# Last pair of a conditioned block: one block product is made last, in PSUM banks of its own, and added to the tokens in two gated parts

## The chip, the cores and the metric

The kernel runs on one core of one Trainium2 chip. The metric is the device time of one execution in microseconds (us). The profile is one execution of its own, and its rows count from the start of its span.

## What is computed

The reference takes 32 batches of 128 tokens with 512 features, a conditioning vector for each batch and a mask. The first half (normalise, modulate, two small networks, gated sum) changes the few masked tokens alone. The second half is for all tokens, and the change lies in it:

```
shift_mlp, scale_mlp, gate_mlp = jnp.split(silu(t) @ ffada_w + ffada_b, 3, axis=1)
ff_norm = _layernorm(x) * (1.0 + scale_mlp[:, None]) + shift_mlp[:, None]
h = gelu(ff_norm @ ff_w1 + ff_b1, approximate=True)      # 512 -> 1024
return x + gate_mlp[:, None] * (h @ ff_w2 + ff_b2)       # 1024 -> 512
```

All of it is float32.

## The kernel before

The tokens are taken in four pairs of groups. A pair p has two sides of four batches: side 0 and side 1. Both matrix products of a pair are done with seven block products instead of eight (Strassen's method in Winograd's form): P1 to P7, with sums and differences of blocks before and after. The first product (512 to 1024) is itself cut into seven such streams, 1, 2, 5, 6, 3, 7, 4, so that a step is named by stream and product: `7P5`. Its results, behind GELU, lie in `ha` (side 0) and `hb` (side 1); each has two halves of the inner dimension.

The second product (`SecondProduct`) has for each column block c (0 or 1, written U and V in the names of steps; 256 token columns, two tiles i of 128 each) two PSUM banks: e (`banks[c][0]`, P5, P2 and P3) and a (`banks[c][1]`, P1, P6, P7 and P4). A step such as `P2V1` is `multiply("P2", 1, 1)`: four matmuls of 128x256 into half a bank. The first half of the output columns of side 0 is bias + P1 + P2, the others are sums of more products:

- `sa`, `se` seed the banks a and e with the bias or its difference; `P1` goes into a, `P5` into e.
- `k5` copies e (P5) out on ScalarE; `ke` copies a (bias + P1) into e; `P2` is added there; e is then the first half of side 0.
- `K00c` copies e to SBUF on ScalarE, `G00c` multiplies it by the gate and `R00c` adds it to the tokens, both on GpSimd (POOL).
- `F`, `B`, `T`, `U` are the operand sums on VectorE. `B` makes the operand of P6. `U` (`fourth_block`) makes the operand of P3, and it overwrites the operand of P2, so that it stands behind P2.
- P3, P7 and P4 are cut a second time into seven inner products, p1 to p7, of 128 columns. Step `5i3` is inner product p5 of P3. `S1` to `S4` are operand sums on POOL, `C` copies on ScalarE, `V` and `J` sums on VectorE. The direct ones (2, 3, 4) go straight into the banks.
- `E0`, `E1`, `E20`, `E21` (`third`) set e to a + P5. Results for side 1 and for the other halves follow: `G11c`, `R11c`, `G10c`, `R10c` on VectorE for side 1, `K01c`, `G01c`, `R01c` on ScalarE and POOL for side 0. In these names the digits are side, half of the columns, c.
- `o00`, `o10` (c, side) store both halves of side 0 from SyncE; `o01`, `o1R`, `o1L` store side 1.

At the very end of the last pair, `4i40` and `4i41` (`last_quarter`) make the last 128 columns for one tile each, in a bank of their own, with a gate, an addition and a store of 64 KB each.

What runs first is an order written out by hand, one for each pair (`ORDER`): the names of the steps in the order in which they are issued. Each engine takes its own instructions in that order and waits by semaphores only where data, a bank or a buffer demands it. Weights for the first product and gates are loaded by SyncE (`W3`, `W4`, `lg0`, `lg1`), in that order too. Behind the last step every engine reads the number of masked tokens left over (`values_load`) and branches past a loop that isn't taken here. `SyncE` then waits for the stores.

Of the kernel before, what the change touches and what calls it, by code (L numbers as in the profile page):

```python
# [9 lines left out]
F32 = mybir.dt.float32  # L10
# [4 lines left out]
ALU = mybir.AluOpType  # L15
# [7 lines left out]
def kernel(  # L23
# [81 lines left out]
    early = ExitStack()  # L105
# [364 lines left out]
    for j, op in enumerate((ALU.is_gt, ALU.is_ge)):  # L470
        nc.gpsimd.affine_select(
            out=upper[:, j],
# [11 lines left out]
        out=lower,  # L484
# [56 lines left out]
    for j in range(2):  # L541
# [4 lines left out]
            start=True,  # L546
            stop=True,
# [34 lines left out]
    for key, vec in (("ssm1", ssm_b1), ("bwd1", bwd_b1), ("ff1", ff_b1)):  # L582
        n = vec.shape[0] // P
# [80 lines left out]
    part = KC // 2  # L664
# [233 lines left out]
    fw2_of = Weights(fw2, HC // 2, D // 2, t_2)  # L898
# [22 lines left out]
    INNER = ("P3", "P7", "P4")  # L921
# [135 lines left out]
    class FirstProduct:  # L1057
# [207 lines left out]
    class SecondProduct:  # L1265
# [55 lines left out]

        def fourth_block(self, c):
            tok, part = self.cols[c], self.ha[:, HC // 2 :]
            nc.vector.tensor_tensor(part[:, :, tok], part[:, :, tok], self.s1[c], ALU.subtract)

        def gated(self, c, side, h, result=None):

# [94 lines left out]
        def last_quarter(self, i):  # L1422

            c = 1
            part = ps_t.tile([P, 512], F32, tag="tr", name=f"last_{i}")[:, :P]
            self.inner[INNER[-1]].multiply("p4", part.unsqueeze(1), True, (i,))
            gate = self.gate[1][:, 2 * c + i, :P]
            nc.vector.tensor_tensor(part, part, gate, ALU.mult)
            xt = self.xs[1][c][:, i, :P]
            nc.vector.tensor_tensor(xt, part, xt, ALU.add)  # L1430
            nc.sync.dma_start(out[(2 * self.p + 1) * G + 2 * c + i, :, :P], xt)

        def store_part(self, lo, hi):
            c = 1
            b = (2 * self.p + 1) * G + 2 * c
            nc.sync.dma_start(
                out[b : b + 2, :, lo:hi].rearrange("b s d -> s b d"), self.xs[1][c][:, :, lo:hi]
            )

    class Inner:  # L1440
# [183 lines left out]
    class Steps:  # L1624
# [14 lines left out]
    def windows(put, q, f, first, last):  # L1639
# [50 lines left out]
        for w in range(first, last):  # L1690
# [70 lines left out]
            ng1121  # L1761
        """,
        3: """
            6P5 5P3 5P7 6P1 5j22 6c5 3P5 6w12 3c5 3P1 6w22 5P4 6s 6P2 5k12 5k21 6k11 6P6 W3 7P5 7P1
            7c5 6e 3w22 6a11 3s 6P7 6P3 6k12 7s 3P2 3P6 3w12 6a12 7P6 7P2 3k11 6j22 7w12 3e 6P4 3P7
            7k11 6a22 7e W4 6j21 4P5 3P3 7P7 7P3 4c5 3k12 F00 6a21 3j22 7w22 4P1 se1 7k12 L11 7j22
            g1222 4s 3P4 7P4 4P2 3j21 L22 se0 4P6 L12 lg0 4w12 7j21 g1221 sa1 F02 4k11 P5U0 g2211 4e
            P5U1 4P7 P1V1 4w22 k50 4j22 L21 sa0 P1U0 g2122 4P4 g2222 4j21 B0 P1U1 g22L 4P3 F12 P1V0
            g2121 ke0 F10 P5V1 4k12 P5V0 B1 T1 k51 P2U0 P2U1 T0 ke1 g2212 P2V0 K000 P2V1 G000 K001
            U0 P6V0 P6U0 R000 lg1 U1 S1i3 5i3 G001 S2i3 1i3 C1i3 S1i7 C5i3 P6V1 6i3 5i7 V6i3 P6U1  # L1770
            C5i7 1i7 C1i7 S3i3 7i3 E0 J30 S2i7 C7i3 R001 S4i3 6i7 2i3 3i3 K010 V7i3 V6i7 S3i7 S1i4
            J70 7i7 S4i7 V7i7 G010 C7i7 5i4 3i7 2i7 E1 J31 1i4 S3i4 S2i4 C1i4 J71 4i3 E20 C5i4 R010
            6i4 K011 S4i4 o00 4i7 G110 R110 V6i4 J40 7i4 E21 V7i4 G111 G011 3i4 C7i4 R011 2i4 J41
            R111 G100 R100 o10 o1R o01 G101 R101 o1L 4i40 4i41
        """,
    }
    seconds, stats = {}, {}
# [1 line left out]
    for p in range(NP):  # L1779
        more_pairs = p + 1 < NP  # L1780
        steps = Steps()
        put = steps.put
# [110 lines left out]
        put("ke0", second.seed_e, 0)  # L1893
        put("B0", second.second_block, 0)
        put_moves(0)
        if p == 0:
# [2 lines left out]
        put_blocks(1)  # L1899
        multiply("P5", 1)  # L1900
        put("k51", second.keep_five, 1)
        put("ke1", second.seed_e, 1)
        put("B1", second.second_block, 1)
        put_moves(1)
        put("T0", second.third_block, 0)
# [36 lines left out]
        join("P7", 0)  # L1942
        direct("P3", "p3")
        second.finish(put, 0, 0, 1, 0)
        put("o00", second.store, 0, 0)
# [5 lines left out]
        put("o10", second.store, 1, 0)  # L1951
        if more_pairs:
            for j in range(1, 5):
                put(f"A{j}", begin, j)
# [10 lines left out]
        put("E21", second.third, 1)  # L1965
        second.finish(put, 1, 1, 1, 0)
        if not more_pairs:
            put("o1R", second.store_part, D // 2, D)
        join("P4", 1)
        next_phases("P5", "P1")  # L1970
        if p + 2 < NP:
# [2 lines left out]
        second.finish(put, 0, 1, 0, 1)  # L1974
        put("o01", second.store, 0, 1)
        next_phases("P2", "P6")
        if more_pairs:
            for n in range(4):
                put(f"nt1{n}", nxt.token_sums, 1, n)
            direct("P4", "p4")  # L1980
            second.finish(put, 1, 1, 0, 1)
            put("o11", second.store, 1, 1)
        else:
            second.finish(put, 1, 1, 0, 1)
            put("o1L", second.store_part, P, D // 2)
            for i in range(2):
                put(f"4i4{i}", second.last_quarter, i)
        if more_pairs:
            put("nW2", nxt.load_weights, 2)
            if p + 2 < NP:  # L1990
# [16 lines left out]
    with tc.If(more > 0):  # L2007
# [11 lines left out]
        with tc.For_i(0, more, 1):  # L2019
# [12 lines left out]
            for half_no, (mod, was, wbs, bias, bcol, func) in enumerate(  # L2032
# [28 lines left out]
                out=out_rows,  # L2061
# [56 lines left out]
```

## Time and profile before

| | us |
|---|---|
| median of 3 runs | 449.38 (448.76 to 450.94) |
| the profiled execution, its own time | 448.01 |
| its span, first to last instruction | 446.3 |
| TensorE busy in the span | 435.6 |
| VectorE, ScalarE, GpSimd busy | 328.0, 205.5, 260.5 |

A row of a timeline or of a chain has the start and the duration in us, the engine (PE is TensorE, PEld its weight loads, DVE VectorE, ACT ScalarE, SP SyncE; a q behind it is that engine's queue), the line of the kernel, and what is written from what. `x8` are eight records; a float32 matmul leaves two. A row of a group has the count, the busy time, the mean ns of one, and the idle time ahead of it with what ended it. A row of a windows table has the length of the stretch, the busy time of PE, PEld, DVE, ACT and POOL, the granted clock of TensorE, and the share and GB/s of the DMA engines.

### The profile page before, as it was taken

What the parts mean: (1) busy time and instruction counts of PE and PEld (TensorE: products, weight loads), DVE (VectorE), ACT (ScalarE), POOL (GpSimd) and SP (SyncE); (2) the same over time, 40 slices, a digit from 0 to 9 for tenths busy, and PEclk for the clock granted to TensorE, in tenths of its full rate; (3) what the DMA queues carried; (4) which work ended last, traced back from release to release, by engine and by line L of the source; (5) the groups of instructions that cost most, each with busy time, mean ns of one, the idle gap of its engine ahead of it and who ended that gap; (6) DMA issues with size and microseconds to landing.
All of it is one profiled execution on the core that took longest, in us unless ns stands there. A gap on an engine that the chain in (4) does not pass through costs nothing.

```text
span 446.3 us, 7040 instructions
## 1 busy us (share of the span) xinstructions
PE 435.6 (98%) x2435; PEld 372.8 (84%) x2435; DVE 328.0 (73%) x592; ACT 205.5 (46%) x453; POOL 260.5 (58%) x226
## 2 busy tenths in 40 slices
PE   8999999999999999999999999999999999999992
PEld 4884684688888999888889998888899988888991
DVE  5788898879998589969762699697627993535174
ACT  3133116353585662536636835356477254652120
POOL 4211470089932895898528927985286618912991
PEclk9999999999999999999999999999999999999997
DMA  7999449895185307741574087416550553311014
GB/s 251 374 395 409 173 88 315 299 359 143 35 182 86 111 1 273 279 141 42 142 166 72 1 296 255 140 41 151 92 135 1 189 189 106 123 29 76 0 49 145
DMA packets 57045, 70.90 MB, mean 159 GB/s; under 512 B 34741, under 2 KB 36109, under 8 KB 55983
## 3 DMA queue, kind: packets, MB, share of 16 engines
q1 hardware_dynamic: 51742, 67.72, 48.1%
q0 software_dynamic: 3008, 2.15, 1.8%
q10 hardware_dynamic: 2256, 0.54, 0.7%
q8 instruction: 21, 0.34, 0.3%
q14 instruction: 18, 0.14, 0.1%
HBM read 56.71 MB, written 13.70 MB: 158 GB/s over the span
## 4 chain that ended last, share of the span: by engine, by line
PE 95%; DVE 2%; POOL 1%; issue 0%; ACT 0%; DVEq 0%
PE a_m L1155 20%; PE e_m L1155 16%; PE a_o L1387 12%; PE e_o L1387 12%; PE one_P L1473 7%; PE po_s L222 6%; PE ph_s L205 5%; PE a_o L1473 4%; PE e_o L1473 2%; PE five_P L1473 2%; PE ph_s L681 2%; PE a_m_alone L1155 1%; PE pm_ss L308 1%; PE pm_f L308 1%; PE part_s L342 0%; PE pl_s L255 0%
## 5 line engine op out<-in xcount | busy, mean ns | idle before, releaser
L1349 POOL TENSOR_TENSOR t<-t,gate 128x512 f32<-128x512 f32 x16 | 23.1, 1444 | 61.4 <-ACT t L1343 57.3
L1182 POOL TENSOR_TENSOR ha<-p_m,ha 128x512 f32<-128x512 f32 x20 | 25.9, 1295 | 48.7 <-DMA tw<-t_rows 23.0
L968 ACT ACTIVATE xT<-xT,modT 128x128 f32<-128x128 f32 x112 | 46.4, 487 | 8.1 <-DMA xT<-xn 8.1
L1207 DVE TENSOR_TENSOR hb<-a_m,hb 128x512 f32<-128x512 f32 x40 | 27.4, 686 | 15.7 <-PE a_m L1155 12.1
L1125 ACT ACTIVATE hb<-hb,biasT 128x256 f32<-128x256 f32 x64 | 28.3, 499 | 15.0 <-DVE hb L1207 14.7
L904 POOL DMA_INDIRECT x<-x_rows,slot_i x24 | 29.3, 1219 | 7.4 <-issue 5.7
L1197 ACT COPY ha<-e_m 128x512 f32<-128x512 f32 x32 | 18.5, 586 | 31.9 <-PE e_m L1155 31.2
L1387 PE MATMUL a_o<-t,s 128*128 128x256 f32 x128 | 29.6, 380 | 0.0
L1387 PE MATMUL a_o<-fw,ha 128*128 128x256 f32 x128 | 29.6, 379 | 0.0
L1387 PE MATMUL e_o<-fw,s 128*128 128x256 f32 x128 | 29.1, 379 | 0.0
L222 PE MATMUL po_s<-w,h_s 128*128 128x512 f32 x64 | 28.4, 594 | 0.0
L1387 PE MATMUL e_o<-fw,ha 128*128 128x256 f32 x128 | 28.3, 379 | 0.0
L1169 ACT COPY p_m<-e_m 128x512 f32<-128x512 f32 x27 | 15.7, 582 | 26.7 <-PE e_m L1155 26.6
L1387 PEld LDWEIGHTS e_o<-fw,ha 128*128 128x128 f32 x128 | 24.4, 190 | 3.3
L1387 PEld LDWEIGHTS e_o<-fw,s 128*128 128x128 f32 x128 | 24.3, 190 | 3.3
L1387 PEld LDWEIGHTS a_o<-fw,ha 128*128 128x128 f32 x128 | 24.4, 190 | 3.3
L1182 POOL TENSOR_TENSOR hb<-p_m,hb 128x512 f32<-128x512 f32 x20 | 26.2, 1313 | 1.5 <-DVE hb L1207 1.2
L1387 PEld LDWEIGHTS a_o<-t,s 128*128 128x128 f32 x128 | 23.7, 191 | 2.9
L1125 ACT ACTIVATE ha<-e_m,biasT 128x256 f32<-128x256 f32 x48 | 20.0, 469 | 12.6 <-PE e_m L1155 12.0
L1398 DVE TENSOR_TENSOR e_o<-a_o,p_o 128x512 f32<-128x512 f32 x16 | 11.0, 695 | 20.1 <-PE a_o L1387 19.0
L1155 PE MATMUL a_m<-xT,tw 128*128 128x256 f32 x96 | 24.6, 379 | 0.0
L1188 DVE TENSOR_TENSOR e_m<-a_m,ha 128x512 f32<-128x512 f32 x20 | 13.9, 696 | 14.5 <-PE a_m L1155 5.1
(275 smaller groups left out, 1151.3 us busy)
## 6 DMA issues: line engine op xcount, KB each, us to landing
x<-in_x_dram SPq DMA_DIRECT2D x16, 512.0 KB, 6.4
tw<-t_rows SPq DMA_DIRECT2D x16, 512.0 KB, 3.6
gate<-gate_rows SPq DMA_DIRECT2D x8, 1024.0 KB
out_dram<-x SPq DMA_DIRECT2D x15, 512.0 KB, 4.4
xT<-xn SPq DMA_DIRECT2D x104, 64.0 KB, 2.1
tw<-t_rows SPq DMA_DIRECT2D x16, 384.0 KB
ada_f<-in_L_cond_ffada_w_dram SPq DMA_DIRECT2D x4, 768.0 KB, 14.7
ada_a<-in_L_cond_ada_w_dram SPq DMA_DIRECT2D x4, 512.0 KB, 3.7
```

The lines of the kernel that those rows point to most:

```text
L205: nc.tensor.matmul(ph[:, :n], w[:, k, ts(f, P)], xT[:, k, :], start=(k == 0), stop=(k == KC - 1))
L222: nc.tensor.matmul(po, h[f][:, ts(i, P)], w[:, f, :], start=(f == 0 and seeded is None), stop=(f == HC - 1), skip_group_check=seeded is no ...
L904: nc.gpsimd.indirect_dma_start(out=xs[i // G][i % G // 2][:, i % 2], out_offset=None, in_=x1_rows, in_offset=bass.IndirectOffsetOnAxis(ap= ...
L968: nc.scalar.activation(out, src, AF.Identity, bias=shift, scale=scale)
L1125: nc.scalar.activation(dst[:, n], src[:, n], AF.Gelu_apprx_tanh, bias=biasT[:, f : f + 1])
L1155: nc.tensor.matmul(bank[:, ts(n, QT)].rearrange("p (i b c) -> p i b c", i=2, c=R), self.w_block(j, product)[:, ts(n, P)], self.x_block(j, ...
L1182: nc.gpsimd.tensor_tensor(self.place(RESULT[j], c), self.p5[j], other, ALU.add)
L1197: nc.scalar.copy(self.place(RESULT[j], c), src)
L1207: nc.vector.tensor_tensor(dst, a, other, ALU.add)
L1349: nc.gpsimd.tensor_tensor(view, view, self.gate[side][:, 2 * c : 2 * c + 2, part], ALU.mult)
L1387: nc.tensor.matmul(bank[:, ts(i, D // 2)], src[:, k, ts(i, P)], w[:, k, :], start=False, stop=True, skip_group_check=True,)
L1473: nc.tensor.matmul(out[:, i % out.shape[1]], src[:, k, ts(i, P)], w[:, k, :], start=(start and (i == 0 or out.shape[1] == 1) and k == 0), ...
```

## The change

It concerns the last pair alone (`NP - 1`); the other pairs issue what they did.

- P2 isn't added to e any more. `ke0` and `ke1` go. In their place `K000` and `K001` copy bias + P1 out of bank a, and `G00c`, `R00c` gate it and add it to the tokens.
- `fourth_block` writes the operand of P3 over that of P1, so that the operand of P2 stays.
- P2 goes into banks of its own (`late`): `P2U0` and `P2U1` into one, `P2V0` and `P2V1` into one each. `H` multiplies by the gate and `M` adds to the tokens, on VectorE: `H00`, `M00` for both tiles of c = 0; `H10`, `M10`, `H11`, `M11` for one tile of c = 1 each.
- The first half of side 0 has stores of its own: `q00` (256 KB) and `q10` (128 KB) from SyncE, `q11` (128 KB) from ScalarE's queue. `o00` and `o10` store the second half, 256 KB each.
- `last_quarter` goes; its product is the direct step `4i4`, and `o1L` stores the whole half.
- The order of the last pair is a new one from its first step on.

```diff
         def fourth_block(self, c):
             tok, part = self.cols[c], self.ha[:, HC // 2 :]
-            nc.vector.tensor_tensor(part[:, :, tok], part[:, :, tok], self.s1[c], ALU.subtract)
+            nc.vector.tensor_tensor(
+                self.operand("P3")[:, :, tok], part[:, :, tok], self.s1[c], ALU.subtract
+            )
...
-                "P1": self.ha[:, :hh], "P2": self.ha[:, hh:], "P3": self.ha[:, hh:],
+                "P1": self.ha[:, :hh], "P2": self.ha[:, hh:],
+                "P3": self.ha[:, :hh] if self.p == NP - 1 else self.ha[:, hh:],
...
+        def late(self, c, i):
+            if c == 0 or i:
+                pool, tag = ((ps_h, "h"), (ps_t, "tr"))[c]
+            else:
+                pool, tag = ps_o, "o"
+            if i == 0 or c:
+                self.own["late", c, i] = pool.tile([P, 512], F32, tag=tag, name=f"late_{c}_{i}")
...
+            for k in range(HC // 2):
+                nc.tensor.matmul(
+                    bank,
+                    src[:, k, ts(i, P)],
+                    w[:, k, :],
...
+        def late_gated(self, c, i):
+            view, gate, _ = self.late_parts(c, i)
+            nc.vector.tensor_tensor(view, view, gate, ALU.mult)
+        def late_added(self, c, i):
+            view, _, xt = self.late_parts(c, i)
+            nc.vector.tensor_tensor(xt, view, xt, ALU.add)
+        def finish_late(self, put, c, i, queue):
+            put(f"H{c}{i}", self.late_gated, c, i)
+            put(f"M{c}{i}", self.late_added, c, i)
+            put(f"q{c}{i}", self.store_part, c, 0, 0, D // 2, (0, 1) if c == 0 else (i,), queue)
...
+        def early(c):
+            if more_pairs:
+                put(f"ke{c}", second.seed_e, c)
+            else:
+                second.finish(put, c, 0, 0, 1)
...
         3: """
...
+            6P5 5P7 6c5 5P3 5j22 3P5 5k12 6w12 6P1 6s 3P1 5P4 6P2 3c5 5k21 6P6 W3 6w22 7P1 6k11 6e
...
+            g2222 P1U1 4e P1U0 se1 4P7 P1V1 P1V0 g22L K000 4j22 4P4 F02 4j21 se0 K001 4P3 P5U1 F12
+            g2122 G000 R000 g2121 P5U0 k50 F10 4k12 P5V0 T0 P5V1 T1 B0 B1 g2212 P6U1 U1 U0 S1i3 P2U0
+            P2U1 5i3 C5i3 S2i3 1i3 C1i3 S1i7 P6V0 5i7 G001 C5i7 lg1 H00 S3i7 R001 6i3 1i7 S2i7 k51
+            P6U0 V6i3 E0 C1i7 P6V1 J30 E1 S3i3 6i7 7i3 S4i3 S4i7 3i3 C7i3 2i3 V6i7 V7i3 J31 7i7 M00
+            V7i7 q00 K010 C7i7 J70 S1i4 4i3 S2i4 5i4 1i4 C1i4 J71 4i7 6i4 K011 E21 C5i4 3i7 G111 2i7
+            V6i4 S3i4 7i4 G011 P2V1 R111 E20 J40 V7i4 G010 C7i4 G110 S4i4 2i4 3i4 R011 J41 o1R 4i4
+            H11 P2V0 R010 o00 R110 M11 G100 R100 G101 o10 q11 R101 H10 M10 o01 o1L q10
```

More of the change, by code (lines that the diff above doesn't have):

```diff
@@ L1420, in join @@
             nc.vector.tensor_tensor(bank, bank, self.inner[product].d[:, c], ALU.add)
[L1422 to L1437, printed above, removed]
+        def late(self, c, i):
[5 more added lines that the diff above has]
+                self.own["late", c, i] = pool.tile([P, 512], F32, tag=tag, name=f"late_{c}_{i}")
+            at = i if c == 0 else 0
+            bank = self.own["late", c, 0 if c == 0 else i][:, ts(at, D // 2)]
+            w = fw2_of.of["P2"]
+            src = self.operand("P2")[:, :, self.cols[c]]
+            for k in range(HC // 2):
[3 more added lines that the diff above has]
+                    w[:, k, :],
+                    start=(k == 0 and at == 0),
+                    stop=True,
+                    skip_group_check=True,
+                )
@@ new lines, in late_parts @@
+        def late_parts(self, c, i):
+            tiles = slice(2 * c, 2 * c + 2) if c == 0 else slice(2 * c + i, 2 * c + i + 1)
+            view = self.own["late", c, i][:, : (tiles.stop - tiles.start) * D // 2]
+            here = slice(tiles.start - 2 * c, tiles.stop - 2 * c)
+            return (
+                view.rearrange("p (i d) -> p i d", d=D // 2),
+                self.gate[0][:, tiles, : D // 2],
+                self.xs[0][c][:, here, : D // 2],
+            )
+        def late_gated(self, c, i):
+            view, gate, _ = self.late_parts(c, i)
+            nc.vector.tensor_tensor(view, view, gate, ALU.mult)
@@ new lines, in late_added, with store_part @@
+        def late_added(self, c, i):
[5 more added lines that the diff above has]
+            put(f"q{c}{i}", self.store_part, c, 0, 0, D // 2, (0, 1) if c == 0 else (i,), queue)
+        def store_part(self, c, side, lo, hi, tiles=(0, 1), queue=nc.sync):
+            b, n = (2 * self.p + side) * G + 2 * c + tiles[0], len(tiles)
+            queue.dma_start(
+                out[b : b + n, :, lo:hi].rearrange("b s d -> s b d"),
+                self.xs[side][c][:, tiles[0] : tiles[0] + n, lo:hi],
@@ L1763 @@
         3: """
[L1764 to L1774, printed above, removed]
+            6P5 5P7 6c5 5P3 5j22 3P5 5k12 6w12 6P1 6s 3P1 5P4 6P2 3c5 5k21 6P6 W3 6w22 7P1 6k11 6e
+            7P5 6P3 6a11 3s 6P7 7c5 3w22 7s 3P2 3w12 7P6 6k12 6j22 6P4 W4 7P2 6a12 3k11 3P6 7k11
+            6j21 6a22 4P5 7w12 7w22 4P1 7e 7P7 3e 7j22 3P7 3j22 7P3 L11 L22 7P4 6a21 lg0 3P3 7k12
+            4c5 L12 4s 7j21 3P4 F00 4w12 L21 3j21 4w22 sa0 4P2 3k12 4k11 sa1 g1222 g2211 4P6 g1221
+            g2222 P1U1 4e P1U0 se1 4P7 P1V1 P1V0 g22L K000 4j22 4P4 F02 4j21 se0 K001 4P3 P5U1 F12
[5 more added lines that the diff above has]
+            H11 P2V0 R010 o00 R110 M11 G100 R100 G101 o10 q11 R101 H10 M10 o01 o1L q10
         """,
@@ L1878, in next_phases, with store_first_side @@
                     nxt.phase(lambda name, *args: put("n" + name, *args), 1, product)
+        def early(c):
[3 more added lines that the diff above has]
+                second.finish(put, c, 0, 0, 1)
+        def store_first_side(c):
+            if more_pairs:
+                put(f"o{c}0", second.store, c, 0)
+            else:
+                put(f"o{c}0", second.store_part, c, 0, D // 2, D)
         put("lg0", second.load_gate, 0)
@@ L1892 @@
         put("k50", second.keep_five, 0)
-        put("ke0", second.seed_e, 0)
+        early(0)
         put("B0", second.second_block, 0)
@@ L1901 @@
         put("k51", second.keep_five, 1)
-        put("ke1", second.seed_e, 1)
+        early(1)
         put("B1", second.second_block, 1)
@@ L1944 @@
         second.finish(put, 0, 0, 1, 0)
-        put("o00", second.store, 0, 0)
+        store_first_side(0)
         apart("P7", "p7")
@@ L1950 @@
         second.finish(put, 1, 0, 1, 0)
-        put("o10", second.store, 1, 0)
+        store_first_side(1)
         if more_pairs:
@@ L1967 @@
         if not more_pairs:
-            put("o1R", second.store_part, D // 2, D)
+            put("o1R", second.store_part, 1, 1, D // 2, D)
         join("P4", 1)
@@ L1976 @@
         next_phases("P2", "P6")
+        direct("P4", "p4")
+        second.finish(put, 1, 1, 0, 1)
         if more_pairs:
@@ L1979 @@
                 put(f"nt1{n}", nxt.token_sums, 1, n)
-            direct("P4", "p4")
-            second.finish(put, 1, 1, 0, 1)
             put("o11", second.store, 1, 1)
         else:
[L1984 to L1987, printed above, removed]
+            put("o1L", second.store_part, 1, 1, 0, D // 2)
+            for c, i, queue in ((0, 0, nc.sync), (1, 0, nc.sync), (1, 1, nc.scalar)):
+                for tile in (i,) if c else range(2):
+                    put(f"P2{'UV'[c]}{tile}", second.late, c, tile)
+                second.finish_late(put, c, i, queue)
         if more_pairs:
```

10 lines of the change are left out of this document (6 added, 4 removed).

## The prediction

> **What bounds the kernel now.** I read the page's first part, then the list of waits of TensorE, then the chain that ended last, and only then the timeline of the last 10 us.
>
> ```profile
> span 446.3 us, 7040 instructions
> PE 435.6 (98%) x2435; PEld 372.8 (84%) x2435; DVE 328.0 (73%) x592; ACT 205.5 (46%) x453; POOL 260.5 (58%) x226
> ...
> PE pm_keep_clock L462 <- DVE zeros L457: 1.3, 1, 1.3
> PE ph_s L681 <- issue: 0.3, 1, 0.3
> PE pl_s L255 <- DVE rank L564: 0.2, 1, 0.2
> ```
>
> TensorE is busy for 98% of the span, and the three waits listed are all that it has, all in the opening. So reordering can't make its stream end sooner; it can only make it end later, by a new wait. What is left to win lies behind its last product. Next, the end of the chain and of the timeline:
>
> ```profile
> 432.10 0.91 PE one_P L1473 x8
> ...
> 433.10 0.44 DVE xn_d L1505
> ...
> 440.47 0.29 DVE x L1430
> ```
>
> ```profile
> 436.40 1.06 PE L1473 MATMUL last<-fw,hb 128*128 128x128 f32 x8
> ...
> 436.95 0.69 DVE L1331 TENSOR_TENSOR a_o<-a_o,gate 128x512 f32<-128x512 f32 x1
> ...
> 439.62 0.29 DVE L1428 TENSOR_TENSOR last<-last,gate 128x128 f32<-128x128 f32 x1
> ...
> 440.26 1.29 SPq L1431 DMA_DIRECT2D out_dram<-x  x2
> 440.47 0.29 DVE L1430 TENSOR_TENSOR x<-last,x 128x128 f32<-128x128 f32 x1
> ```
>
> The chain leaves TensorE at 433.0 and runs on VectorE, without a gap, from 433.10 to 440.76, though TensorE ends at 437.46. VectorE is 3.3 us behind: work for gating and adding piles up there while TensorE still has products whose results nobody can use sooner. SyncE's last two stores end their issue at 441.55. Behind them:
>
> ```profile
> L2007 SPq EVENT_SEMAPHORE  x7: 17/17/17, 442.8 to 444.6; - x7
> ...
> L2113 SPq EVENT_SEMAPHORE  x14: 17/28/28, 444.7 to 446.2; - x14
> ...
> 438.00:439.00 1.00, 0.00 (x0) 0.00 (x0) 0.98 (x2) 0.00 (x0) 0.00 (x0) 1.00 0.92 336
> ...
> 441.00:442.00 1.00, 0.00 (x0) 0.00 (x0) 0.00 (x0) 0.00 (x0) 0.00 (x0) 0.50 1.00 339
> 442.00:443.00 1.00, 0.00 (x0) 0.00 (x0) 0.00 (x0) 0.00 (x0) 0.00 (x0) 0.50 0.53 159
> 443.00:444.00 1.00, 0.00 (x0) 0.00 (x0) 0.00 (x0) 0.00 (x0) 0.00 (x0) 0.50 0.13 28
> ```
>
> SyncE waits for the stores until 444.6 and closes at 446.2. From the end of the last issue to the end of the span: 446.3 - 441.55 = 4.75 us. In the windows the last two columns are DMA share and GB/s: the stores flow at 336 to 339 GB/s, most are through by about 442.6, and after 443 a share of 0.13 is left, some two of 16 engines running behind.
>
> **The change part by part.** Durations for it:
>
> ```profile
> 401.44 10.36 PE e_o L1387 x48
> ...
> 422.28 2.68 PE one_P L1473 x24
> ...
> L1505 DVE TENSOR_TENSOR xn_d<-one_P,xn_d 128x256 f32<-128x256 f32 x6 | 2.6, 425 | 9.5 <-PE one_P L1473 8.7 <-ACT xn_d L1500 0.8
> L1324 DVE TENSOR_TENSOR ha<-ha,s 128x1024 f32<-128x1024 f32 x2 | 2.5, 1246 | 2.3 <-PE e_o L1387 2.3
> L1338 DVE TENSOR_TENSOR x<-a_o,x 128x512 f32<-128x512 f32 x2 | 1.4, 692 | 0.1
> L1331 DVE TENSOR_TENSOR a_o<-a_o,gate 128x512 f32<-128x512 f32 x2 | 1.4, 690 | 0.0
> L1311 DVE TENSOR_TENSOR s<-s,ha 128x1024 f32<-128x1024 f32 x1 | 1.2, 1224 | 4.7 <-PE e_o L1387 4.7
> L1343 ACT COPY t<-e_o 128x512 f32<-128x512 f32 x4 | 2.3, 586 | 7.0 <-PE e_o L1387 4.4 <-POOL hb L1462 2.4 <-PE e_o L1473 0.2
> L1500 ACT COPY xn_d<-five_P 128x256 f32<-128x256 f32 x3 | 1.1, 377 | 2.9 <-PE five_P L1473 2.9
> L1462 POOL TENSOR_TENSOR si_P<-ha 128x512 f32<-128x512 f32 x1 | 1.3, 1265 | 1.2 <-DVE ha L1324 1.2
> ```
>
> A step of P1 to P7 here is 8 matmul records: 10.36/6 = 1.73 us at 256 columns, 2.68/3 = 0.89 us in the inner products.
>
> *TensorE's total.* P2 keeps its four steps (16 matmuls), and the two halves of the last quarter become one direct step with the same 8 records. Nothing is added: cost 0, and the end stays at 437.46, unless there is a wait.
>
> *P2 goes behind.* In the new order TensorE ends with 2i7, 7i4, P2V1, 2i4, 3i4, 4i4, P2V0. Counted back from 437.3 (437.46 less about 0.17 for the modelled end of the last record) the steps end: P2V0 437.3, 4i4 435.6, 3i4 434.7, 2i4 433.8, P2V1 432.9, 7i4 431.2, 2i7 430.3. So the quarter of P4 that came last is there 1.7 us sooner, and VectorE works on it while P2V0 runs.
>
> *VectorE's end.* Operations start 0.6 to 0.7 us apart, halves 0.43; results of TensorE are usable 0.2 us after its step. E20 waits for 2i7: 430.5. Then J40 431.1, V7i4 431.7, G110 432.2, J41 432.8, H11 433.4, R110 433.8, M11 434.4, G100 434.9 (3i4 is there at 434.9), R100 435.65, G101 436.3, R101 437.0, H10 437.6 (P2V0 is there at 437.5), M10 438.0, done 438.46. Added are H00, M00 (2 x 0.69) and H11, M11, H10, M10 (4 x 0.43); the four of 0.29 go. H00 and M00 come near 410 and 423, where nothing waits for them. So VectorE ends 2.3 us sooner (440.76 - 438.46) with 1.9 us more to do.
>
> *SyncE's end.* M10 lets go of the last store at 438.5, its issue ends at 438.9, against 441.55: 2.6 us sooner. The other part of that tile, q11, is issued by ScalarE at about 434.9, behind its last copy; nothing waits behind it. On SyncE q00 waits from about 418 for M00, and behind it there is only o1R, due at 430.4. o00 waits for R010 (434.1); o10, o01 behind it come at 434.6 and 436.4.
>
> *The stores.* The bytes are the same. From 434 on there are 1.57 MB left (two of 256 KB, q11, o01 of 512 KB, o1L of 256 KB, q10): at 339 GB/s 4.6 us, from 435 to 439.7, with the last store issued at 438.5. So the queue is no longer behind than before, and I let 4.75 us follow the last issue as before; its bounds are in the rivals.
>
> *Copies on ScalarE.* ke0 and ke1 go (0.57 each), the copy for the first half is taken from the bank of P1 instead. POOL's G000 and R000 move to about 394.
>
> *The fourth block* goes into P1's operand: the same VectorE instruction, 1.25 us. It waits no more for P2, but for second and third block, which stand ahead of it on VectorE.
>
> *The first 30 us of the pair* have a new order, with the same steps. I laid both orders out, each engine in its order, each step starting when its operands are there. The old order laid out in this way ends VectorE at 441.1 (trace 440.76). In the new one no step of TensorE is late. Weights: the first half for stream 7 is asked for 0.9 us later, needed at the same 371.9, and has 1 us to spare, as stream 4's had before. The narrowest places are these:
>
> ```profile
> 409.05 1.69 POOL L1349 TENSOR_TENSOR t<-t,gate 128x512 f32<-128x512 f32 x1 [17.17 <-ACT t L1343]
> ...
> 408.38 1.23 DVE L1324 TENSOR_TENSOR ha<-ha,s 128x1024 f32<-128x1024 f32 x1
> ...
> 430.15 1.06 PE L1473 MATMUL one_P<-t,hb 128*128 128x128 f32 x8
> ...
> 431.30 0.37 ACT L1500 COPY xn_d<-one_P 128x256 f32<-128x256 f32 x1 [2.80 <-PE one_P L1473]
> ...
> 431.94 1.06 PE L1473 MATMUL one_P<-t,si_P 128*128 128x128 f32 x8
> ```
>
> (a) 1i7 waits for the copy C5i7 with one inner step between: 0.89 - 0.17 - 0.07 - 0.38 - 0.07 = 0.2 us to spare. The old 6i4 stood just so behind C1i4 (copy done at 431.67, product at 431.94), and TensorE did not wait. (b) 5i3 waits for S1i3. Between P5 and 5i3 there were P2 and two steps of P6, 10.3 us; now there are three steps, 5.18 us. The chain in them: 0.24 + B1 1.22 + U1 1.25 + 0.07 + S1i3 1.27 + 0.07 = 4.1 us, 1.06 us to spare. (c) S4i4 stands on POOL behind G011 and G010, which wait for K011: done at 431.6, needed at 433.8. POOL's idle 17.17 us ahead of 409.05 takes in G000 and R000.
>
> *Sum.* 0 on TensorE, -2.6 us at the last issue. The profiled execution took 448.01 us (span 446.3 and 1.7 around it): 445.4. It lies 1.4 us below the median of the runs, 449.38; there the forecast is 446.8 us, -0.58%. The likeliest case's own range is 445.9 to 447.8.
>
> **The rivals.**
>
> *A. The end of the stores eats the gain.* For: the DMA share of 0.13 after 443; the bytes, not the issue, end last.
>
> ```profile
> q1 hardware_dynamic: 1648, 2.10, 27.8%
> q8 instruction: 3, 0.05, 1.1%
> ```
>
> These are packets and MB after 425: three instruction loads of about 16 KB stand among the stores, each on one engine: 16 KB at 339/16 = 21 GB/s is 0.77 us. If two more of them fall in front of the last store on one engine, 1.5 us of 2.6 are gone: 448.3. Against: the stores are spread wider now (q00 goes at 423).
>
> *B. The engines that run behind catch up.* Then the landing follows the last issue by the 1.1 us that most bytes needed (441.55 to about 442.6) rather than 3.1 (to 444.6): up to 2 us more, 444.8. [...]
>
> *C. TensorE waits, and it gets slower.* The place is 5i3, where P2's cover is halved. The chain B1, U1, S1i3 has 1.06 us to spare; every us that it grows beyond that costs 1 us. Grown by 3.7 us it has eaten the gain, by 5.9 us (a stall of 4.85) the kernel is clearly slower: 451.7. U0 is on VectorE while S1i3 runs on POOL, and the row at 409.05 shows a POOL operation at 1.69 instead of 1.27 us beside such a block: 0.43 of the 1.06 us. [...] Held up for the whole of U0 (1.25 us), 5i3 would be late by 0.2 us: 447.0. Against more than that: all three instructions have their rows above, and B1 waits only for P5.
>
> *D. Nothing moves*, because VectorE still ends last in the end: that needs 2.3 us more on it after 430, five operations of 0.43; the order has none. 449.4.
>
> **How the numbers follow.** Forecast 0.60, A 0.20, B 0.09, C 0.06, D 0.05. What a measurement can tell from no change is about 0.5%, 2.25 us: 447.1. The forecast lies only 0.3 us below it, so of its 0.60 I count 0.44 as faster and 0.16 as the same; B is faster. Faster 0.53, same 0.41 (with A and D), slower 0.06. The range takes in the forecast, B's lower end, A and the edge of D: 444.6 to 449.6.
>
> **What would show it.** TensorE's last record near 437.5 and no wait on it after the opening; VectorE's last operation 1.0 us behind it rather than 3.3; SyncE's last issue near 438.9; its waits over near 442. Wrong if TensorE's list of waits shows 5i3, 1i7 or 7P1 waiting, or if the waits for the stores still end past 443.5.

## The result and the profile after

The changed kernel takes 445.57 us (median of 6 runs, 445.35 to 446.57); the kernel before, beside it on the same chip, 449.35 (448.62 to 450.94). The ratio is 0.9918, with a 95% interval from 0.9899 to 0.9937: 3.8 us or 0.8% faster. Compared again on another chip (below) the ratio is 0.9939, 0.9926 to 0.9952: 2.8 us. The forecast was 446.8 us, 2.6 us faster, with a range from 444.6 to 449.6. The first comparison has 6 runs of before, whose median of 449.35 lies 0.7 to 0.9 us above the medians of 17 or 23 runs in the later ones (448.42 to 448.65), so that the 3.8 us may be in part a slow draw of before.

The profiled execution took 445.40 us, its span is 443.7. First the page's first part and the waits of TensorE in the changed kernel:

```profile
span 443.7 us, 7035 instructions
PE 435.8 (98%) x2435; PEld 372.3 (84%) x2435; DVE 329.8 (74%) x594; ACT 203.7 (46%) x451; POOL 260.3 (59%) x226
...
PE pm_keep_clock L462 <- DVE zeros L457: 1.3, 1, 1.3
PE ptr L974 <- DVE xn L861: 0.4, 1, 0.4
PE ph_s L681 <- issue: 0.3, 1, 0.3
PE pl_s L255 <- DVE rank L564: 0.2, 1, 0.2
```

TensorE has as many records and the same busy time to 0.2 us; VectorE has two operations more and is busy for 1.8 us longer. There is one new wait, of 0.4 us, in the opening (L974), in code that the change does not touch. No step of the new order waits. Then the chain's end and the timeline's:

```profile
431.96 1.73 PE late L1438 x8
433.69 1.80 PE a_o L1511 x16
...
438.27 0.35 DVE late L1460
438.64 0.42 DVE x L1464
```

```profile
435.31 1.06 PE L1511 MATMUL a_o<-fw,hb 128*128 128x128 f32 x8
435.35 0.39 ACTq L1473 DMA_DIRECT2D out_dram<-x  x1
...
436.20 1.89 PE L1438 MATMUL late<-fw,ha 128*128 128x256 f32 x8
437.58 0.69 DVE L1340 TENSOR_TENSOR x<-a_o,x 128x512 f32<-128x512 f32 x1
438.18 0.42 DVE L1460 TENSOR_TENSOR late<-late,gate 128x256 f32<-128x256 f32 x1
438.30 1.27 SPq L1473 DMA_DIRECT2D out_dram<-x  x2
438.64 0.42 DVE L1464 TENSOR_TENSOR x<-late,x 128x256 f32<-128x256 f32 x1
```

The chain stays on TensorE until 435.5, where before it left at 433.0. While `P2V0` runs (from 436.20) VectorE gets as far as `R101`, which it starts at 437.58; only `H10` and `M10` come behind it, and VectorE is done at 439.06, 0.97 us behind TensorE's 438.10. SyncE's waits for the stores and the last windows:

```profile
L2060 SPq EVENT_SEMAPHORE  x7: 17/17/17, 440.7 to 442.0; - x7
...
L2166 SPq EVENT_SEMAPHORE  x14: 17/28/28, 442.0 to 443.6; - x14
...
438.00:439.00 1.00, 0.10 (x1) 0.00 (x0) 0.96 (x3) 0.00 (x0) 0.00 (x0) 1.00 1.02 380
439.00:440.00 1.00, 0.00 (x0) 0.00 (x0) 0.07 (x1) 0.00 (x0) 0.00 (x0) 1.00 0.99 333
440.00:441.00 1.00, 0.00 (x0) 0.00 (x0) 0.00 (x0) 0.00 (x0) 0.00 (x0) 0.87 0.46 156
441.00:442.00 1.00, 0.00 (x0) 0.00 (x0) 0.00 (x0) 0.00 (x0) 0.00 (x0) 0.50 0.15 42
```

From the end of the last issue (439.57) to the end of the span 4.1 us pass, where it was 4.75.

To compare executions, the next table counts the end from TensorE's last product, and gives ahead of it when the opening is over (the start of the first product of pair 0, L1155) and how long TensorE takes from one fixed record, number 2000 counted from 0, to its end; both kernels issue the same up to there. All in us, each from one profiled execution.

| kernel | opening over | record 2000 to TensorE's end | VectorE done | last issue done | SyncE's waits over | span ends |
|---|---|---|---|---|---|---|
| before | 81.36 | 76.55 | +3.30 | +4.09 | +7.13 | +8.83 |
| changed | 81.96 | 76.55 | +0.97 | +1.47 | +3.88 | +5.58 |

The products of the last pair take the same time to 0.01 us. Behind TensorE 3.25 us are gone: 2.62 up to the last issue, 0.63 behind it. The semaphore updates that the traces keep, which no view prints, show where the 0.63 us lie. Each store leaves 16 updates of its semaphore, as many as the page counts DMA engines, and I read them as one from each. Before, 14 of them had come for the last store at +5.45, and in the changed kernel 15 at +2.85: 1.36 and 1.38 us behind the last issue, so most of the bytes are no sooner. In both kernels the last of SyncE's waits ended with the 16th update of the store ahead of the last one: at +7.11 before, at +3.87 in the changed kernel, 3.02 and 2.40 us behind the last issue. So the 0.63 us lie in the update that comes last, by my reading the DMA engine that ends last. The span is only 2.6 us shorter because the opening ended 0.6 us later in this execution. In the profiled executions of the experiments it ends between 81.78 and 83.73, whatever the kernel, so the before's was the earliest of all; this is part of the scatter of the times.

### The profile page after: what moved, and what is told of

It is laid out like the page before. It is cut to its first block, busy times and chain, and to the rows that moved or that the text cites. A ratio compares the mean times of both kernels' runs of the same rounds, so it can differ in the third digit from the quotient of the medians.

```text
span 443.7 us, 7035 instructions
## 1 busy us (share of the span) xinstructions
PE 435.8 (98%) x2435; PEld 372.3 (84%) x2435; DVE 329.8 (74%) x594; ACT 203.7 (46%) x451; POOL 260.3 (59%) x226
## 4 chain that ended last, share of the span: by engine, by line
PE 76%; DMA 8%; DVE 8%; issue 3%; POOL 2%; ACT 1%; SPq 0%; POOLq 0%; DVEq 0%; ACTq 0%
PE a_m L1155 18%; PE e_m L1155 14%; PE a_o L1390 12%; PE e_o L1390 11%; PE one_P L1511 7%; PE a_o L1511 4%; DMA fw<-in_L_cond_ff_w_dram 3%; PE po_s L222 3%; DMA w<-in_L_cond_bwd_w_dram 3%; PE e_o L1511 2%; PE five_P L1511 2%; DMA x_wide<-t_s 2%; PE late L1438 1%; DVE t L403 1%; PE a_m_alone L1155 1%
## 5 line engine op out<-in xcount | busy, mean ns | idle before, releaser
L1155 PE MATMUL a_m<-xT,tw 128*128 128x256 f32 x96 | 24.5, 379 | 0.0
L1155 PE MATMUL e_m<-s,fw 128*128 128x256 f32 x92 | 23.7, 380 | 0.0
L222 PEld LDWEIGHTS po_s<-w,h_s 128*128 128x128 f32 x64 | 11.8, 191 | 13.1 <-issue 12.9
L1155 PE MATMUL a_m<-xT,t 128*128 128x256 f32 x88 | 22.4, 379 | 0.0
```

The costliest lines, as they stand in the source:

```text
L222: nc.tensor.matmul(po, h[f][:, ts(i, P)], w[:, f, :], start=(f == 0 and seeded is None), stop=(f == HC - 1), skip_group_check=seeded is no ...
L1155: nc.tensor.matmul(bank[:, ts(n, QT)].rearrange("p (i b c) -> p i b c", i=2, c=R), self.w_block(j, product)[:, ts(n, P)], self.x_block(j, ...
```

## The experiments

The theory (the first in the expectations): VectorE's backlog behind TensorE has gone, since the last product is one whose result needs only a gate and an addition, and the others run beneath it. The rival: the gain comes from the stores, since 256 KB (`q00`) and the other parts leave sooner and the queue is emptier at the end. A third question is how near the new order is to a wait.

| kernel | median, us | ratio to before (95%) | record 2000 to end | VectorE | last issue | span ends |
|---|---|---|---|---|---|---|
| e5, changed, again | 445.86 | 0.9939 (0.9926 to 0.9952) | 76.55 | +0.97 | +1.49 | +5.57 |
| e3, before, half stored early | 448.84 | 1.0009 (0.9998 to 1.0020) | 76.55 | +3.30 | +4.05 | +9.30 |
| e12, before, `o01` in halves | 448.36 | 0.9998 (0.9986 to 1.0011) | 76.55 | +3.30 | +3.67 | +8.07 |
| e2, `q00` joined to `o00` | 445.87 | 0.9946 (0.9930 to 0.9961) | 76.55 | +0.97 | +2.12 | +6.25 |
| e10, `q11` on SyncE | 445.47 | 0.9926 (0.9913 to 0.9940) | 76.55 | +0.97 | +1.34 | +5.46 |
| e7, stores sooner | 445.43 | 0.9943 (0.9925 to 0.9961) | 76.55 | +0.97 | +1.39 | +5.33 |
| e1, all of P2 early | 447.92 | 0.9991 (0.9975 to 1.0007) | 78.16 | +1.90 | +2.65 | +6.16 |
| e6, the same, `H10`, `M10` moved | 448.60 | 0.9995 (0.9981 to 1.0009) | 77.44 | +1.90 | +2.57 | +8.00 |
| e9, `P2V0` alone early | 447.67 | 0.9983 (0.9973 to 0.9993) | 76.55 | +1.90 | +2.30 | +7.63 |
| e11, e9 with e7's stores | 446.60 | 0.9962 (0.9947 to 0.9977) | 76.55 | +1.90 | +2.30 | +6.15 |
| e8, half of the cover gone | 447.49 | 0.9984 (0.9969 to 0.9998) | 78.27 | +0.97 | +1.46 | +5.56 |
| e4, all of it gone | 450.60 | 1.0049 (1.0032 to 1.0066) | 81.65 | +0.97 | +1.47 | +5.59 |

The medians of before in these comparisons are 448.42 to 448.65.

**e5: the changed kernel again, on another chip.**

> The changed kernel once more, beside the kernel before on this chip and in its own profile. Theory 1, with the opening's chance taken off: from TensorE's last product to the end of the span 5.6 us (before 8.8), the last pair itself as long as before; the opening differs from run to run by up to 2 us and has no part in it. So 3.2 us faster than before, a ratio near 0.993. If the opening were part of the change, its first product of the first pair would come late again, at 82.0 or more against 81.4.

The end is the same to 0.02 us. The opening is over 0.5 us later still (82.50), with a wait that the other execution does not have:

```profile
PE e_m L1155 <- DMA tw<-t_rows: 1.0, 1, 1.0
```

That execution took 447.12 us and the others of the same kernel down to 445.39: waits ahead of the last pair move single executions by more than a microsecond.

**e3: the kernel before, with half of side 0 stored early.** The first half of side 0 leaves as soon as `R000` and `R001` have added to it, near 413 and 423.

```diff
+                if self.p == NP - 1 and side == 0 and h == 0:
+                    put(f"q{c}", self.store_half, c, 0)
...
         def store(self, c, side):
+            if self.p == NP - 1 and side == 0:
+                return self.store_half(c, 1)
```

> The kernel before, with the first halves of side 0 stored as soon as they are added (near 412 and 422), and second halves where both were stored: 512 KB less in the last 14 us, nothing else moved. Theory 1: VectorE still ends 3.3 us behind TensorE; at most the last issue's wait in the queue and the engines that run behind come in, 0.3 to 0.9 us faster than before: 448.5 to 449. Theory 2: most of the gain is there, 446.5 or less.

512 KB less stand in the queue at the end and nothing is gained: 1.0009, and the span ends 9.30 behind TensorE against 8.83. The rival falls: early stores alone bring nothing while VectorE is late.

**e12: the kernel before, with `o01` (512 KB) cut into halves**, the second half of the columns stored once `R110` is done.

```diff
-        put("o01", second.store, 0, 1)
+        if more_pairs:
+            put("o01", second.store, 0, 1)
+        else:
+            put("o0R", second.store_half, 0, D // 2, D)
+            put("o0L", second.store_half, 0, 0, D // 2)
```

> The kernel before, with o01 stored in halves: the right one as soon as it is added (near 432.6), the left one in the old place, so that 256 KB less stand in front of the last stores; VectorE is as before, 3.3 us behind TensorE. If bytes in front of the last stores are a part of the gain: the span ends 8.0 to 8.4 us behind TensorE instead of 8.8, 0.4 to 0.8 us faster than before. If only the last issue counts: 8.7 to 8.9 us.

The last issue is done 0.4 us sooner and the profiled end is 0.76 us sooner, as expected, but the times show no difference (0.9998, give or take 0.13%, or 0.6 us). What it is worth stays open; it is no large part of the change's 3 us.

**e2: `q00` joined to `o00`**, so that the two halves of one column block leave in one store of 512 KB at the end, as before.

```diff
-            put(f"q{c}{i}", self.store_part, c, 0, 0, D // 2, (0, 1) if c == 0 else (i,), queue)
+            if c:
+                put(f"q{c}{i}", self.store_part, c, 0, 0, D // 2, (i,), queue)
...
-                put(f"o{c}0", second.store_part, c, 0, D // 2, D)
+                put(f"o{c}0", second.store_part, c, 0, (0, D // 2)[c], D)
```

> The changed kernel without q00: o00 stores both halves of its tile in one transfer of 512 KB, as before the change, so that 256 KB more leave after 434. Theory 1: the last store is issued at the same time, up to 0.4 us lost in the queue behind it: 445.6 to 446.0. Theory 2: most of the gain goes, 447.5 or more.

The profiled end is 0.67 us later, all of it in the last issue; the times (0.9946) cannot be told from the changed kernel's.

**e10: `q11` from SyncE instead of ScalarE's queue.**

```diff
-            for c, i, queue in ((0, 0, nc.sync), (1, 0, nc.sync), (1, 1, nc.scalar)):
+            for c, i, queue in ((0, 0, nc.sync), (1, 0, nc.sync), (1, 1, nc.sync)):
```

> The changed kernel with q11 issued by SyncE, in its place in the order, instead of ScalarE. SyncE issues q11 near 437.5 less 1.5 us, behind o10, with o01 due 1.3 us later: the last issue stays where it is, no change beyond 0.3 us. If the second queue is what makes the last stores land sooner: the end is 0.5 us or more farther from TensorE's last product than 5.6 us.

Nothing changes (0.9926, the end at +5.46): the second queue brings nothing.

**e7: the changed kernel, `o10` ahead of `o00` and `o01` in two halves.**

```diff
-            H11 P2V0 R010 o00 R110 M11 G100 R100 G101 o10 q11 R101 H10 M10 o01 o1L q10
+            H11 P2V0 R010 o10 o00 R110 o0R M11 G100 R100 G101 q11 R101 H10 M10 o0L o1L q10
```

> The changed kernel with o10 ahead of o00 on SyncE, and o01 stored in two halves, the right one as soon as it is added: 512 KB leave about 1.8 us sooner, into a stretch from 433 to 435 in which no store runs. If bytes still in the queue set the landing of the last store: the end is 0.4 to 0.7 us nearer to TensorE's last product (5.6), 0.1% faster than the changed kernel. If the landing follows the last issue, no change beyond 0.2 us.

0.25 us sooner in the profile, less than expected, and no difference in the times. No kernel here is clearly better than the changed one.

**e1 and e6: all of P2 early**, next to `P2U0` and `P2U1`, with one bank for each c; gate, addition and store of c = 1 go with it. In e1 `H10` and `M10` both stand behind `V7i7`; e6 (shown) has them at other places on VectorE.

```diff
-            P2U1 5i3 C5i3 S2i3 1i3 C1i3 S1i7 P6V0 5i7 G001 C5i7 lg1 H00 S3i7 R001 6i3 1i7 S2i7 k51
+            P2U1 P2V0 P2V1 5i3 C5i3 S2i3 1i3 C1i3 S1i7 P6V0 5i7 G001 C5i7 lg1 H00 H10 S3i7 R001 6i3 1i7 S2i7 k51
...
-            V7i7 q00 K010 C7i7 J70 S1i4 4i3 S2i4 5i4 1i4 C1i4 J71 4i7 6i4 K011 E21 C5i4 3i7 G111 2i7
-            V6i4 S3i4 7i4 G011 P2V1 R111 E20 J40 V7i4 G010 C7i4 G110 S4i4 2i4 3i4 R011 J41 o1R 4i4
-            H11 P2V0 R010 o00 R110 M11 G100 R100 G101 o10 q11 R101 H10 M10 o01 o1L q10
+            V7i7 q00 K010 C7i7 J70 S1i4 4i3 S2i4 5i4 1i4 C1i4 J71 M10 q10 4i7 6i4 K011 E21 C5i4 3i7 G111 2i7
+            V6i4 S3i4 7i4 G011 R111 E20 J40 V7i4 G010 C7i4 G110 S4i4 2i4 3i4 R011 J41 o1R 4i4
+            R010 o00 R110 G100 R100 G101 o10 R101 o01 o1L
```

> All of P2 keeps its banks of its own and its two gated parts, but P2V0 and P2V1 stand behind P2U1, 5 us after P5, and their gate, addition and one store of 256 KB come near 424; the last product is 4i4 again. Theory 1 (the gain is VectorE's backlog behind the last product): TensorE ends no later, VectorE ends about 2.7 us behind it (changed kernel 1.0, before 3.3), the span ends about 7.3 us behind TensorE (5.6 and 8.8): some 1.7 us slower than the changed kernel, 447.3. Theory 2 (the gain is that stores leave earlier): the stores leave even earlier here, so no slower than the changed kernel, 445.6 or less.

> As the kernel with P2 early, but with H10 ahead of V6i3 and M10 behind J71, where VectorE has room, so that TensorE's direct steps of P7 need not wait for J71. Theory 1: no wait on TensorE, the last pair as long as in the changed kernel; VectorE ends 2.5 to 2.9 us behind TensorE, the span 7.1 to 7.5 us behind it: 1.5 to 1.9 us slower than the changed kernel. Theory 2 (stores): as fast as the changed kernel or faster, since 256 KB more leave early.

The gain is gone in both (0.9991, 0.9995), more than was expected. TensorE waits, for 1.1 us in e1 and 0.6 in e6, and its stretch is 1.61 and 0.89 us longer. The profiled ends are not where theory 1 had them: +6.16 in e1 (7.3 was expected) and +8.00 in e6 (7.1 to 7.5). The timeline of e6, with its row of the list of waits first:

```profile
PE a_o L1508 <- DVE a_o L1423: 0.6, 1, 0.6
...
434.37 1.06 PE L1508 MATMUL one_P<-t,hb 128*128 128x128 f32 x8
434.57 0.70 DVE L1401 TENSOR_TENSOR e_o<-a_o,p_o 128x512 f32<-128x512 f32 x1 [0.27 <-PE a_o L1508]
435.31 0.70 DVE L1423 TENSOR_TENSOR a_o<-a_o,xn_d 128x512 f32<-128x512 f32 x1
436.06 2.05 PE L1508 MATMUL a_o<-t,hb 128*128 128x128 f32 x16 [0.63 <-DVE a_o L1423]
...
440.22 0.69 DVE L1340 TENSOR_TENSOR x<-a_o,x 128x512 f32<-128x512 f32 x1
```

`2i4` goes into bank a, which `E20` reads and `J40` adds to first. `E20` needs `2i7`, so 1.5 us of VectorE lie between two direct products, and only `7i4` (0.89 us) is left between them. `P2V1` was what covered this. At the end VectorE is done 1.90 us behind TensorE, not 3.30: this part of the shorter backlog needs no late P2.

**e9: `P2V0` alone early, `P2V1` where the change has it.** This takes the wait away and leaves only what the last place of `P2V0` brings.

```diff
-            P2U1 5i3 C5i3 S2i3 1i3 C1i3 S1i7 P6V0 5i7 G001 C5i7 lg1 H00 S3i7 R001 6i3 1i7 S2i7 k51
+            P2U1 P2V0 5i3 C5i3 S2i3 1i3 C1i3 S1i7 P6V0 5i7 G001 C5i7 lg1 H00 H10 S3i7 R001 6i3 1i7 S2i7 k51
...
-            V7i7 q00 K010 C7i7 J70 S1i4 4i3 S2i4 5i4 1i4 C1i4 J71 4i7 6i4 K011 E21 C5i4 3i7 G111 2i7
+            V7i7 q00 K010 C7i7 J70 S1i4 4i3 S2i4 5i4 1i4 C1i4 J71 M10 q10 4i7 6i4 K011 E21 C5i4 3i7 G111 2i7
...
-            H11 P2V0 R010 o00 R110 M11 G100 R100 G101 o10 q11 R101 H10 M10 o01 o1L q10
+            H11 R010 o00 R110 M11 G100 R100 G101 o10 q11 R101 o01 o1L
```

> The changed kernel with P2V0 alone made early (behind P2U1; H10 behind H00, M10 and its store behind J71); P2V1 stays between 7i4 and 2i4, where it covered the chain 2i7, E20, J40, 2i4, on which TensorE waited 0.6 us with both parts early. The last product is 4i4. Theory 1: no wait on TensorE, the last pair as long as in the changed kernel (76.55 us from a fixed matmul of it); VectorE ends 1.9 us behind TensorE (changed kernel 0.97), the last issue 2.3 to 2.4 us (1.5), the span 6.4 to 6.6 us (5.6): 0.9 us slower than the changed kernel. If the cover of P2V1 were all that counts: as fast as the changed kernel. If both parts have to be late: 2.5 us slower.

TensorE does not wait in the last pair, VectorE is done at +1.90 and the last issue at +2.30, as expected; but the end is at +7.63, a microsecond later than that allows. The kernel loses some 2.0 us of the change's gain instead of 0.9. The timeline and the windows of e9 show what lies between:

```profile
437.59 1.06 PE L1511 MATMUL a_o<-fw,hb 128*128 128x128 f32 x8
439.25 0.62 SPq L1371 DMA_DIRECT2D out_dram<-x  x1
439.86 0.69 DVE L1340 TENSOR_TENSOR x<-a_o,x 128x512 f32<-128x512 f32 x1
440.58 0.37 SPq L1473 DMA_DIRECT2D out_dram<-x  x1
...
441.00:442.00 1.00, 0.00 (x0) 0.00 (x0) 0.00 (x0) 0.00 (x0) 0.00 (x0) 0.50 1.01 358
442.00:443.00 1.00, 0.00 (x0) 0.00 (x0) 0.00 (x0) 0.00 (x0) 0.00 (x0) 0.50 0.62 206
443.00:444.00 1.00, 0.00 (x0) 0.00 (x0) 0.00 (x0) 0.00 (x0) 0.00 (x0) 0.50 0.09 26
```

`o01`, 512 KB, is issued at 439.25, only 1.3 us ahead of the last store (440.58), so that the last one's bytes may have to wait behind it.

**e11: e9 with the stores of e7.** If those bytes are the cause, they go with `o01` in two halves.

```diff
-            H11 R010 o00 R110 M11 G100 R100 G101 o10 q11 R101 o01 o1L
+            H11 R010 o10 o00 R110 o0R M11 G100 R100 G101 q11 R101 o0L o1L
```

> The kernel with P2V0 early ended 7.6 us behind TensorE, not 6.5, though its last issue came where expected: o01 (512 KB) is issued 0.6 us behind TensorE's end there (changed kernel 1.1 us ahead of it), and o1L right behind it. Here o10 goes ahead of o00 and the right half of o01 leaves as soon as it is added, so that 256 KB less stand in front of the last store. If bytes in the queue made up the missing 1.1 us: the span ends 6.5 to 6.9 us behind TensorE, 0.7 to 1.1 us faster than with P2V0 early. If it is one engine running behind for another reason: 7.4 to 7.6 us.

Same last issue (+2.30), end at +6.15 instead of +7.63, and 0.9962 instead of 0.9983, 1.0 us. The two intervals overlap slightly (0.9973 to 0.9977). In e11 256 KB are issued 1.3 us ahead of the last store, in e9 512 KB. The same windows in e11:

```profile
441.00:442.00 1.00, 0.00 (x0) 0.00 (x0) 0.00 (x0) 0.00 (x0) 0.00 (x0) 0.50 0.73 265
442.00:443.00 1.00, 0.00 (x0) 0.00 (x0) 0.00 (x0) 0.00 (x0) 0.00 (x0) 0.50 0.16 44
```

So the stores make e9's excess, as the expectation for bytes had it. That it is the bytes just ahead of the last store is not shown, and e1 speaks against it. Its last two stores are those of e9, 512 KB and then 256 KB 1.3 us later:

```profile
442.08 0.37 SPq L1371 DMA_DIRECT2D out_dram<-x  x1
443.41 0.71 SPq L1470 DMA_DIRECT2D out_dram<-x  x1
```

Its last issue is even done later than e9's (+2.65), and yet its span ends at +6.16, like e11's. Its times agree: less the 1.61 us by which TensorE's stretch is longer, its ratio would be about 0.9955, an estimate, near e11's 0.9962 and not e9's 0.9983. e1 does not have the 128 KB of `q11`, which e9 issues some 1.6 us ahead of `o01`. Of the last store's 16 semaphore updates 14 had come at +4.38 in e9 and at +4.09 in e11, but the last one came at +6.24 and +4.72 (+5.12 in e1). Most of the difference lies in the one or two updates, by my reading DMA engines, that come last, and what makes them late stays open.

e11 and e7 differ in the place of `P2V0` and of its gate, addition and store: VectorE 0.93 us later, end 0.82 us later in the profiles, and some 0.9 us in the ratios (0.9962 against 0.9943, whose intervals overlap).

**e8 and e4: the cover of `5i3` taken away.** e8 moves `P2U1`, e4 both `P2U0` and `P2U1`, from ahead of `5i3` to behind `P6V1`. e4 is shown.

```diff
-            g2122 G000 R000 g2121 P5U0 k50 F10 4k12 P5V0 T0 P5V1 T1 B0 B1 g2212 P6U1 U1 U0 S1i3 P2U0
-            P2U1 5i3 C5i3 S2i3 1i3 C1i3 S1i7 P6V0 5i7 G001 C5i7 lg1 H00 S3i7 R001 6i3 1i7 S2i7 k51
-            P6U0 V6i3 E0 C1i7 P6V1 J30 E1 S3i3 6i7 7i3 S4i3 S4i7 3i3 C7i3 2i3 V6i7 V7i3 J31 7i7 M00
+            g2122 G000 R000 g2121 P5U0 k50 F10 4k12 P5V0 T0 P5V1 T1 B0 B1 g2212 P6U1 U1 U0 S1i3
+            5i3 C5i3 S2i3 1i3 C1i3 S1i7 P6V0 5i7 G001 C5i7 lg1 S3i7 R001 6i3 1i7 S2i7 k51
+            P6U0 V6i3 E0 C1i7 P6V1 P2U0 P2U1 J30 E1 H00 S3i3 6i7 7i3 S4i3 S4i7 3i3 C7i3 2i3 V6i7 V7i3 J31 7i7 M00
```

> As the kernel with the cover gone, but P2U0 stays ahead of 5i3 and P2U1 alone goes behind P6V1. In the changed kernel S1i3 took 2.18 us beside U0 and ended 0.17 us ahead of 5i3; without P2U1, 1.73 us less stands ahead of 5i3, so that TensorE waits about 1.6 us. If a wait costs its own length: the last pair is 1.6 us longer. With the cover wholly gone a wait of 3.2 us made it 5.1 us longer, with the granted clock at 0.5 for some 3.5 us after it; if the clock falls after any wait of this kind: 2.5 us or more longer. [...]

> The changed kernel with P2U0 and P2U1 moved from ahead of 5i3 to behind P6V1 (H00 behind E1). This tests the prediction's place (b): between P5 and 5i3 stands only P6U1, 1.73 us, for a chain B1, U1, S1i3 of 4.1 us. Expected by that chain: TensorE waits 2.4 us at 5i3, the kernel is 2.4 us slower than the changed one, 448.0. Rival: the POOL sum is stretched beside U0 as the row at 409.05 was, then 2.8 us, 448.4. If the chain had more to spare than worked out, less than 2 us.

In e8 TensorE waits for 1.45 us and the stretch grows by 1.72. In e4 it waits for 3.17 us, where 2.4 and with the rival 2.8 were expected, and the stretch grows by 5.10. The list of waits, `5i3`, and the windows of e4 behind it, where the column ahead of the last two is the granted clock:

```profile
PE five_P L1511 <- POOL si_P L1500: 3.2, 1, 3.2
...
411.13 1.16 PE L1511 MATMUL five_P<-fw,si_P 128*128 128x128 f32 x8 [3.17 <-POOL si_P L1500]
...
412.00:413.00 1.00, 1.00 (x8) 1.00 (x7) 0.00 (x0) 0.37 (x1) 1.00 (x2) 0.59 0.00 0
413.00:414.00 1.00, 1.00 (x6) 1.00 (x6) 0.00 (x0) 0.00 (x0) 1.00 (x2) 0.50 0.06 16
414.00:415.00 1.00, 1.00 (x3) 0.79 (x3) 0.00 (x0) 0.37 (x1) 1.00 (x2) 0.50 0.00 0
415.00:416.00 1.00, 1.00 (x5) 0.79 (x4) 0.00 (x0) 0.00 (x0) 1.00 (x1) 0.71 0.00 0
```

And in e8:

```profile
411.30 1.16 PE L1511 MATMUL five_P<-fw,si_P 128*128 128x128 f32 x8 [1.45 <-POOL si_P L1500]
...
412.00:413.00 1.00, 1.00 (x12) 1.00 (x11) 0.00 (x0) 0.37 (x1) 1.00 (x2) 1.00 0.00 0
```

After the wait of 3.17 us the granted clock was at half, from about 1 us behind the first product (411.13) on. Worked out from the windows, 0.59 is 0.82 us at half and 0.71 is 0.58 us: 0.82 + 1 + 1 + 0.58 = 3.4 us, in which 1.7 us of work are lost. 3.17 + 1.7 = 4.9 of the 5.10 us. What is left, 0.2, is about what the stretch grew beyond the wait where the clock stayed whole, 0.26 in e6 and 0.27 in e8. In e6 the windows show a granted clock of 1.00 through the wait and to TensorE's end (434 to 439), and in e8 through the wait of 1.45 us and behind it (405 to 420). No run has a wait between 1.45 and 3.17 us in the last pair, and why the clock fell after the one and not after the other is not shown.

## Why the prediction was right, point by point

- *TensorE's total, no wait.* Right: the stretch of the last pair is 76.55 us in both. The forecast of its end, 437.46, was missed by 0.6 us because the opening took longer in this execution.
- *VectorE's end.* Right: 1.0 us behind TensorE was forecast, 0.97 measured, in every kernel whose last step is `P2V0`. The experiments split the 2.33 us: 1.40 go with the rest of the change, not taken apart further (e9 and e6 stand at 1.90), 0.93 with the last place of `P2V0`.
- *The last issue.* Right: 2.6 us forecast, 2.62 measured against TensorE's end.
- *What follows the last issue.* This is the term that was mis-sized: taken as 4.75 us, it is 4.1. The single profiles give 0.63 us more gain than the sum, 3.25 in all; the medians give 3.8 and 2.8. It was taken as unchanged since the bytes are the same. For most of the bytes that held (1.36 and 1.38 us behind the last issue); what shrank is how far the DMA engine that ends last lags behind (3.02 and 2.40 us). That is the mechanism of rival B, which put up to 2 us on it. Why that engine lagged less is not shown. The bytes issued shortly ahead of the last store don't explain it alone: e9 and e11 have the last issue at the same +2.30 and end 1.5 us apart, but e1, with e9's last two stores, ends like e11. The joined store of e2 costs 0.67 us, but in the issue, and e12 moves the profiled end and not the times.
- *The stores are not the limit* (rival A). Right for this change: nothing of the gain was eaten, and e3, e7 and e10 show that sooner stores or a second queue bring nothing that the times can tell. It is no rule: e9 ends about a microsecond later than e11, which differs from it in the stores alone.
- *The narrow places.* (a) and (c) held: neither is in TensorE's list of waits. (b) held by far less than was forecast. The rows of the changed kernel:

```profile
406.89 2.36 DVE L1324 TENSOR_TENSOR ha<-ha,s 128x1024 f32<-128x1024 f32 x2
407.09 3.62 PE L1438 MATMUL late<-fw,ha 128*128 128x256 f32 x16
408.19 2.18 POOL L1500 TENSOR_TENSOR si_P<-ha 128x512 f32<-128x512 f32 x1 [10.65 <-DVE ha L1324]
410.54 1.05 PE L1511 MATMUL five_P<-fw,si_P 128*128 128x128 f32 x8
```

`S1i3` took 2.18 us, not the 1.27 of the row of before, and ended at 410.37: 0.17 us ahead of `5i3`, where 1.06 were forecast to spare. It ran beside `U0` (the second of the two operations in 406.89). Rival C named this and allowed for 0.43 us, from the row of 1.69; it was 0.91.
- *Rival C's price*, 1 us for each us of wait, held to 0.3 us in e8 (1.72 for 1.45) and failed in e4 (5.10 for 3.17), where the granted clock fell to 0.50. 5.9 us of growth was named as the point where the kernel is clearly slower. In e4 the kernel is slower than before by 0.5% with a wait of 3.17 us, where 4.85 had been put.
- *Rival D* fell: VectorE has no five operations more at the end.
- What the working did not see: that `P2V1` covers `E20` and `J40` ahead of `2i4`. It stands in the order it laid out, and so the sum is right. Without it TensorE waits 0.63 us and its stretch is 0.89 us longer (e6 against e9), and with `P2V0` early as well nothing is left of the gain.

## What to carry to other kernels

Where one engine is busy throughout, look at what still runs behind its last instruction, and give the last place to the product whose result needs the least work; its own time then covers the work on the others. Moving such a piece out of the middle takes cover from there, so count the chain beneath each place it leaves, with the durations that operations have beside their neighbours (`S1i3` beside `U0`: 2.18 us, where 1.27 had been put). Judge the stores by when the last DMA engine has them in, and try more than one arrangement: neither the bytes taken out of the end (e3) nor those just ahead of the last store (e1 against e9) told it here.

## What the runs showed of the hardware that was not expected

- `S1i3` on GpSimd (`si_P<-ha`, 128x512) took 2.18 us in the changed kernel and 2.17 in e4 and e8, each time beside `U0` on VectorE (`ha<-ha,s`, 128x1024); the same operation took 1.27 in before, at 413.24, with nothing on VectorE beside it. In about 1.1 us of overlap it lost 0.9.
- In e4 the granted clock of TensorE was 0.50 for about 3.4 us (worked out from the windows), from about 1 us behind the product that ended a wait of 3.17 us. In e8, with a wait of 1.45 us, it was 1.00 in every window from 405 to 420.
- Of the 16 semaphore updates of the last store 15 come well ahead of the last one: 0.65 us in the profile of before (6.61 and 7.26 us behind TensorE's end), 1.23 in the changed kernel (2.85 and 4.08), 0.95 in e9 (5.29 and 6.24). The last of SyncE's waits ended with the last update of one of the last two stores: at 7.11, 3.87 and 6.24. So in these profiles a store's median landing time would be too short a figure for the tail. What makes that update late was not tried.
